# Graph attention on one core: another order for the first batch and another end for the last

## The chip, the core and the metric

The kernel runs on one core of one Trainium2 chip. The metric is device time in microseconds, the median over runs of the same program. Engines are named as in the profile: PE is the matmul engine (TensorE) and PEld its weight loads, DVE is VectorE, ACT is ScalarE, POOL is GpSimd, and SP is the engine that here only issues transfers.

## The reference

There are 16 batches (B) of 1024 rows (N) with 256 features (D), and an adjacency matrix for each batch, 0 or 1 as drawn here and symmetric. Two layers follow each other, each with a residual and a layernorm:

```python
# layer 0, for entries of adj that are 1 (the others give sigmoid(-max) = 0)
e     = leaky_relu(einsum('bid,bjd->bij', x * a0, x), 0.2)
alpha = where(adj == 1, sigmoid(e), 0)
x     = layernorm(x + alpha @ x + bias)
# layer 1
H = x @ W;  s = H @ a[:256];  d = H @ a[256:]
e = where(adj != 0, exp(-leaky_relu(s[:, None] + d[None, :], 0.2)), 0)
x = layernorm(x + elu((e @ H) / rowsum(e)))
```

## The kernel before

The work for one batch is cut into 8 tiles of 128 rows. A batch passes through two slots of the program: in slot b the kernel makes the scores and the layer 0 sum of batch b, and the layer 1 sum of batch b - 1. The order of the instructions is written out by hand (the scheduler is off), so each engine takes its instructions in the order of the Python text, and waits only for data and for buffers.

For layer 0 the score matrix before masking is symmetric, so only its upper part is multiplied. `strip(b, jt)` multiplies the rows of tile jt with all columns from tile jt on (PE, line 208), in chunks of at most 512 columns; ACT applies two tanh to each chunk (lines 216 and 217) and DVE keeps the greater (line 218) in `tb`. `finish(b, jt, c0, c1)` masks the strip with the adjacency (DVE, line 224) and adds 2 on the diagonal block (POOL, line 234), which carries the residual. The lower part comes from the upper one. In batch 0 `mirror(b, jt)` does it by transposes on PE (line 263) that DVE reads from PSUM and masks (line 265); in later batches `dump`, `gather` and `mask` do it by a DVE transpose and two transfers over DRAM. `sum0(b, t)` multiplies the masked scores with x for tile t (line 315), and DVE evicts the sum and takes its statistics (lines 323, 276 and 277). After four tiles `center` makes the reciprocal root of the variance with a power and one Newton step on POOL (lines 283 to 300), and `scale0` normalizes the rows on ACT (line 304).

Layer 1 needs the normalized rows transposed. `save_x1` writes half of them to DRAM, `fetch_x1` reads them back in blocks by eight transfers (line 113), and `turn_x1` finishes the transpose on DVE (line 352). `project` multiplies with W (line 376), extended by two columns that `make_Wx` computes from W and a (lines 165 and 166). `weights(b, m)` makes one row block e of the attention (DVE, line 420), `sum1` multiplies it (PE, line 427), `elu` and `add` make the elu, the residual and the statistics (lines 443 to 456), `scale1` normalizes and `store` writes out.

For batch 0 the transposed x comes from PE: `transpose_x` transposes x (line 189), DVE copies the result (line 191) and ACT multiplies a second copy by a0 (`acol`, line 192). For the other batches `load_blocks` reads x in blocks (eight transfers on SP) and `turn_x` finishes on DVE (line 179) and ACT (line 180). The buffer of batch 1's transposed x is the one that held `a_bc`, which `make_Wx` reads.

PSUM is cut into three pools: `ps_e` (3 buffers, the score chunks), `ps_t` (2 buffers, transposes) and `ps_acc` (3 buffers, sums).

In the first slot of the kernel before, all four transposes of x by halves come first, then strips 0 to 3 with their mirrors 0 to 3, then `make_Wx`, and then the sums, each followed by one of strips 4 to 7. Transfers are issued by SP (x, the blocks, DRAM traffic and stores) and by POOL (the adjacency, which changes type on the way).

At the end of the last batch, tiles 0 to 3 of layer 1 are summed together as the weights become ready, then tiles 4 to 7 one by one. The last three tiles' roots are taken on POOL. Before the last store each engine reads a flag that says whether the data had only zeros and ones in the adjacency (line 659); if so, it jumps over a second, general program (line 1005), and the engines meet at the end (line 1040).

Of the kernel before, what the change touches and what calls it, by code (L numbers as in the profile page):

```python
# [9 lines left out]
F32 = mybir.dt.float32  # L10
# [4 lines left out]
ALU = mybir.AluOpType  # L15
# [3 lines left out]
P = 128  # L19
# [10 lines left out]
def one_kind_pass(  # L30
# [53 lines left out]

    def load_x(b, pieces=1):
        xs[b] = two.tile([P, NT, D], F32, tag="x", name=f"x_{b}")
        rows = x[b].rearrange("(t p) d -> p t d", p=P)
        n = NT // pieces
        for g in range(pieces):
            nc.sync.dma_start(xs[b][:, ts(g, n), :], rows[:, ts(g, n), :])  # L90

# [37 lines left out]


    acol = const.tile([P, ND], F32, tag="acol", name="acol")
    with nc.allow_non_contiguous_dma(reason="a column of 256"):
        nc.sync.dma_start(acol, a0.rearrange("(c p) o -> p (c o)", p=P))
    load_x(0, 2)
    ident = const.tile([P, P], F32, tag="ident", name="ident")
# [3 lines left out]
    minus1 = const.tile([P, 1], F32, tag="minus1", name="minus1")  # L139
    nc.vector.memset(minus1, -1.0)  # L140
    ones = const.tile([P, 1], F32, tag="ones", name="ones")
    nc.vector.memset(ones, 1.0)
# [16 lines left out]

    def make_Wx():  # L160

        for c in range(ND):
            wprod = one.tile([P, 2, D], F32, tag="tmp", name=f"wprod_{c}")
            for s in range(2):
                nc.vector.tensor_tensor(wprod[:, s, :], Wx[:, c, 2:], a_bc[:, ts(s, D)], ALU.mult)
            nc.vector.tensor_reduce(Wx[:, c, 0:2], wprod, AX.X, ALU.add)

# [13 lines left out]

    def transpose_x(b, g, c):
        if g == 0 and c == 0:
            new_xT(b)
            xas[b] = one.tile([P, ND, N], F32, tag="xa", name=f"xa_{b}")
        pool, tag = (ps_t, "t") if g == 0 else (ps_e, "e")
        pt = pool.tile([P, HT, P], F32, tag=tag, name=f"pxT_{b}_{g}_{c}")
        for t in range(HT):
            nc.tensor.transpose(pt[:, t, :], xs[b][:, g * HT + t, ts(c, P)], ident)  # L189
        flat = pt.rearrange("p t q -> p (t q)")  # L190
        nc.vector.tensor_copy(xTs[b][:, c, ts(g, HALF)], flat)
        nc.scalar.mul(xas[b][:, c, ts(g, HALF)], flat, acol[:, c : c + 1])

# [112 lines left out]
    x1s, mv0s, r0s = {}, {}, {}  # L306

    def sum0(b, t):
        if t == 0:
            x1s[b] = two.tile([P, NT, D], F32, tag="x1", name=f"x1_{b}")  # L310
            mv0s[b] = small.tile([P, NT, 2], F32, tag="mv0", name=f"mv0_{b}")
            r0s[b] = []
        acc = ps_acc.tile([P, D], F32, tag="acc", name=f"acc0_{b}_{t}")
        for jt in range(NT):
            nc.tensor.matmul(  # L315
                acc,
                lhsT=als[b][:, jt, ts(t, P)],
                rhs=xs[b][:, jt, :],
                start=(jt == 0),
                stop=(jt == NT - 1),  # L320
            )
        y = x1s[b][:, t, :]
        nc.vector.scalar_tensor_tensor(y, acc, 0.5, bias_bc, ALU.mult, ALU.add)  # L323
        stats(y, mv0s[b][:, t, :], f"0_{b}_{t}")
        if t % HT == HT - 1:
            g = t // HT
            r0s[b] += center(mv0s[b][:, ts(g, HT), :], f"0_{b}_{g}")
# [107 lines left out]
    def elu(b, t, acc):  # L435
# [10 lines left out]
        if (b, t) == (B - 1, NT - 1):  # L446
            nc.vector.tensor_scalar(hs[b, t], acc[:, 0:D], rinv, 0.0, ALU.mult, ALU.max)
        else:
            nc.scalar.activation(hs[b, t], acc[:, 0:D], AF.Relu, scale=rinv)  # L449
        nc.scalar.activation(ys[b][:, t, :], acc[:, 0:D], AF.Exp, scale=rinv)  # L450

    def add(b, t):

        y = ys[b][:, t, :]
        nc.vector.scalar_tensor_tensor(y, y, 1.0, hs[b, t], ALU.min, ALU.add)
        nc.vector.scalar_tensor_tensor(y, y, -1.0, x1s[b][:, t, :], ALU.add, ALU.add)
        stats(y, mv1s[b][:, t, :], f"1_{b}_{t}")
# [3 lines left out]

    def store(b, t0, n):
        rows = out[b].rearrange("(t p) d -> p t d", p=P)
        nc.sync.dma_start(rows[:, ds(t0, n), :], ys[b][:, ds(t0, n), :])

# [4 lines left out]

    for g in range(2):
        for c in range(ND):
            transpose_x(0, g, c)
    strip(0, 0)
    for jt in range(HT):
        if jt < HT - 1:
            strip(0, jt + 1)
        finish(0, jt, 0, HALF)
        mirror(0, jt)
    make_Wx()  # L480
    load_x(1)
    new_xT(1)
    load_blocks(xTs[1], x[1], 0, N)
    for t in range(NT):
        sum0(0, t)
        if t < HT:
            finish(0, t, HALF, N)
            strip(0, t + HT)
        if 1 <= t <= HT:
            finish(0, t + HT - 1)  # L490
            if t < HT:
                mirror(0, t + HT - 1)
        if t in (4, 5):
            scale0(0, 2 * t - 8)
            scale0(0, 2 * t - 7)
        if t == 5:
            save_x1(0, 0)
            fetch_x1(0, 0)
        if t in (5, 6):
            turn_x(1, t - 5)  # L500
        if t < CHECKS:
            check_adj(0, t)

    for b in range(1, B):
# [29 lines left out]
        if not last:  # L534
            load_x(b + 1)
            new_xT(b + 1)
            load_blocks(xTs[b + 1], x[b + 1], 0, N)
# [24 lines left out]
        for t in range(NT):  # L562
# [8 lines left out]
            if last and t == 7:  # L571
                weights(b, 1)
            if t >= 1:
# [24 lines left out]
    last, done = B - 1, B - 2  # L598
    r1s[last] = []
    n_first = 4  # L600
    first = [acc1(last, t, *((ps_e, "e") if t < 3 else (ps_t, "t"))) for t in range(n_first)]
    for m in range(NT):
        if m >= 2:
            weights(last, m)
# [14 lines left out]
    for t in range(NT):  # L619
# [9 lines left out]
        elu(last, t, acc)  # L629
        if 1 <= t < NT - 1:  # L630
            add(last, t - 1)
        if t == 5:
            nc.vector.tensor_copy(flag, total)
        if t == 6:
            add(last, t)
        if t in (4, 6):
            r1s[last] += center(mv1s[last][:, ds(0 if t == 4 else 3, 3), :], f"1_{last}_{t}")
        if t == 6:
            r1s[last] += center(mv1s[last][:, 6:7, :], f"1_{last}_6")
        for q in range(2 * t - 6, 2 * t - 4) if 3 <= t < 7 else []:  # L640
            scale1(done, q)
            if q in (3, 7):
                store(done, q - 3, HT)
        if t == 6:
            for q in range(3):
                scale1(last, q)
            store(last, 0, 3)

    t = NT - 1
    add(last, t)  # L650
    for q in range(3, t):
        scale1(last, q)
        if q == 5:
            store(last, 3, 3)
        elif q == 6:
            store(last, 6, 1)
    mv = mv1s[last][:, t : t + 1, :]
    r = rstd(mv, f"1_{last}_{t}")
    n_bad = nc.values_load(
        flag, min_val=0, max_val=P, skip_runtime_bounds_check_because="a number of partitions"  # L660
    )
    y = ys[last][:, t, :]
    nc.vector.tensor_scalar(y, y, mv[:, 0, 0:1], r, ALU.subtract, ALU.mult)
    store(last, t, 1)
    return n_bad
# [378 lines left out]
```

## Time and profile before

| | us |
|---|---|
| median of 3 runs | 1286.6 |
| lowest and highest of them | 1285.33, 1298.05 |
| the profiled execution, its own time | 1284.06 |
| span of its trace | 1282.3 |
| PE busy | 1258.7 (98%) |
| DVE, ACT, POOL busy | 923.6, 651.9, 294.5 |
| first transpose on PE starts | 5.39 |
| first strip on PE starts | 8.54 |
| first strip of the second slot starts | 56.86 |
| last store is issued | 1273.74 |

The span runs from the first to the last instruction of the program; the profiled execution's own time is 1.8 us longer, for what lies around it. Times in the trace count from the start of the span. A row of the timeline gives the start, the duration, the engine, the line, the operation and its tiles, how many were merged, and in brackets how long the engine had been idle and what ended the wait. A letter q behind an engine's name means its sequencer, which issues transfers and handles waits and jumps.

### The profile page before, as it was taken

To read this page: it belongs to the slowest core of one execution; us is meant where nothing else is said; L and a number is where in the kernel's file an instruction comes from. 1 tells how busy PE (TensorE), PEld (TensorE's weight loads), DVE (VectorE), ACT (ScalarE), POOL (GpSimd) and SP (SyncE) were. 2 spreads that over 40 slices of the span, in tenths; PEclk is the share of its full clock that TensorE was granted. 3 is DMA by queue.
4 is the path that set the end of the run, shared out by engine and by line. 5 is a ranking of instruction groups with operands and counts; after the bars stand their busy time and mean duration, and the time that the engine had idled before them with its cause. 6 is when DMAs were issued, how large, how long until landed. Compare 5 with 4: busy or idle time off the path is not lost.

```text
span 1282.3 us, 17435 instructions
## 1 busy us (share of the span) xinstructions
PE 1258.7 (98%) x5453; PEld 1021.8 (80%) x5453; DVE 923.6 (72%) x1999; ACT 651.9 (51%) x1461; POOL 294.5 (23%) x606
## 2 busy tenths in 40 slices
PE   7999999999999999999999999999999999999995
PEld 5778787887878878788787878878788787887884
DVE  5585877858678686886868768686786868768564
ACT  4544545457354564544545444564545645446424
POOL 2212231212212122221222312222121221212213
PEclk9999999999999999999999999999999999999998
DMA  9388484885948769386694858958487593866201
GB/s 215 69 176 147 88 199 89 178 177 100 200 84 193 147 130 197 75 184 138 140 207 89 194 95 176 179 104 190 90 194 153 123 198 77 190 137 135 81 16 69
DMA packets 604421, 180.25 MB, mean 141 GB/s; under 512 B 481960, under 2 KB 586912, under 8 KB 604320
## 3 DMA queue, kind: packets, MB, share of 16 engines
q1 hardware_dynamic: 583728, 137.56, 49.3%
q0 software_dynamic: 20592, 41.48, 18.3%
q8 instruction: 46, 0.75, 0.2%
q14 instruction: 55, 0.45, 0.1%
HBM read 151.91 MB, written 60.62 MB: 166 GB/s over the span
## 4 chain that ended last, share of the span: by engine, by line
PE 93%; issue 4%; POOL 1%; DVE 0%; DMA 0%; ACT 0%; SPq 0%; POOLq 0%
PE acc L315 34%; PE acc L427 30%; PE pe L208 19%; PE pH L376 8%; POOL r L285 1%; DMA x<-in_x 0%; PE pxT L189 0%; PE pal L263 0%; POOL ve L283 0%; DVE e L420 0%; PE prow L402 0%; POOL mr L300 0%; POOL n L288 0%; POOL n L289 0%; POOL n L290 0%
## 5 line engine op out<-in xcount | busy, mean ns | idle before, releaser
L427 PE MATMUL acc<-H,e 128*128 128x257 f32 x2048 | 448.8, 380 | 0.6 <-DVE e L420 0.6
L315 PE MATMUL acc<-x,al 128*128 128x256 f32 x2048 | 445.5, 379 | 0.0
L427 PEld LDWEIGHTS acc<-H,e 128*128 128x128 f32 x2048 | 387.7, 189 | 58.5 <-DVE e L420 1.3
L315 PEld LDWEIGHTS acc<-x,al 128*128 128x128 f32 x2048 | 387.6, 190 | 52.6 <-issue 0.5
L208 PE MATMUL pe<-xa,xT 128*128 128x384 f32 (+3 forms) x768 | 267.5, 486 | 0.0
L208 PEld LDWEIGHTS pe<-xa,xT 128*128 128x128 f32 x768 | 141.5, 189 | 86.4 <-issue 45.5
L304 ACT ACTIVATE x<-x,mr,r 128x256 f32<-128x256 f32 x128 | 69.2, 592 | 224.5 <-POOL mr L300 224.5
L420 DVE SCALAR_TENSOR_TENSOR e<-p,pq,adj 128x1024 f32<-128x1024 f32 x128 | 159.7, 1270 | 19.3 <-DMA p<-p_row 16.3
L283 POOL TENSOR_SCALAR ve<-mv 128x4 f32<-128x4 f32 (+3 forms) x51 | 17.8, 349 | 677.2 <-DVE mv L277 671.9
L449 ACT ACTIVATE h<-acc,rinv 128x256 f32<-128x256 f32 x127 | 59.7, 470 | 185.7 <-DVE rinv L444 168.1
L216 ACT ACTIVATE tb<-pe 128x512 f32<-128x512 f32 (+1 forms) x192 | 94.3, 491 | 111.5 <-PE pe L208 81.2
L443 DVE TENSOR_SCALAR rinv<-acc 128x1 f32<-128x1 f32 x128 | 20.1, 157 | 160.7 <-PE acc L427 160.7
L121 ACT ACTIVATE junk<-adj,minus 128x2048 bf16<-128x2048 bf16 x64 | 127.4, 1990 | 0.0
L218 DVE TENSOR_TENSOR tb<-tb,low 128x512 f32<-128x512 f32 (+1 forms) x192 | 103.6, 545 | 32.5 <-ACT low L217 32.1
L376 PE MATMUL pH<-Wx,x1T 128*128 128x258 f32 x512 | 126.6, 381 | 0.0
L376 PEld LDWEIGHTS pH<-Wx,x1T 128*128 128x128 f32 x512 | 97.2, 190 | 36.0 <-issue 14.3
L234 POOL TENSOR_TENSOR al<-ident,al 128x128 f32<-128x128 f32 x128 | 68.0, 531 | 225.6 <-DVE al L224 225.3
L224 DVE SCALAR_TENSOR_TENSOR al<-tb,adj 128x512 f32<-128x512 f32 (+7 forms) x132 | 97.5, 738 | 5.0
L323 DVE SCALAR_TENSOR_TENSOR x<-acc,bias_bc 128x256 f32<-128x256 f32 x128 | 53.9, 421 | 57.9 <-PE acc L315 57.8
L217 ACT ACTIVATE low<-pe 128x512 f32<-128x512 f32 (+1 forms) x192 | 93.0, 485 | 0.0
L255 DVE SCALAR_TENSOR_TENSOR al<-al,adj 128x512 f32<-128x512 f32 (+3 forms) x150 | 76.4, 534 | 20.6 <-DMA al<-mir 20.6
L240 DVE STREAM_TRANSPOSE tb<-tb 128x896 f32<-128x896 f32 (+6 forms) x105 | 74.7, 712 | 3.6
(66 smaller groups left out, 904.4 us busy)
## 6 DMA issues: line engine op xcount, KB each, us to landing
adj<-in_adjT POOLq DMA_DIRECT2D x30, 1024.0 KB, 9.5
x_rows<-x SPq DMA_DIRECT2D x31, 512.0 KB, 3.5
x1T<-x_rows SPq DMA_DIRECT2D x248, 64.0 KB, 2.5
x<-in_x SPq DMA_DIRECT2D x15, 1024.0 KB, 5.9
xT<-in_x SPq DMA_DIRECT2D x120, 128.0 KB, 3.4
out<-y SPq DMA_DIRECT2D x30, 512.0 KB, 4.3
p<-p_row POOLq DMA_DIRECT2D x15, 512.0 KB, 4.5
mir<-tb SPq DMA_DIRECT2D x60, 112.0 KB, 2.4
```

Of the source, the lines that this page charges most:

```text
L121: nc.scalar.activation(junk, rows, AF.Square, bias=minus1, scale=2.0, accum_out=chk[:, b * CHECKS + n : b * CHECKS + n + 1],)
L208: nc.tensor.matmul(pe[:, 0:w], lhsT=xTs[b][:, c, ts(jt, P)], rhs=xas[b][:, c, ds(jt * P + o, w)], start=(c == 0), stop=(c == ND - 1),)
L216: nc.scalar.activation(tb[:, ds(o, w)], pe[:, 0:w], AF.Tanh, scale=0.5)
L217: nc.scalar.activation(low[:, 0:w], pe[:, 0:w], AF.Tanh, scale=0.5 * SLOPE)
L218: nc.vector.tensor_tensor(tb[:, ds(o, w)], tb[:, ds(o, w)], low[:, 0:w], ALU.max)
L224: nc.vector.scalar_tensor_tensor(als[b][:, jt, c0:c1], tbs[b, jt][:, c0 - jt * P : c1 - jt * P], 1.0, adjs[b, jt // HT][:, jt % HT, c0:c1] ...
L240: nc.vector.transpose(tb, tb)
L255: nc.vector.scalar_tensor_tensor(v, v, 1.0, rows, ALU.add, ALU.mult)
L315: nc.tensor.matmul(acc, lhsT=als[b][:, jt, ts(t, P)], rhs=xs[b][:, jt, :], start=(jt == 0), stop=(jt == NT - 1),)
L376: nc.tensor.matmul(pt, lhsT=x1Ts[b][:, c, ts(t, P)], rhs=Wx[:, c, :], start=(c == 0), stop=(c == ND - 1),)
L420: nc.vector.scalar_tensor_tensor(es[b][:, m, :], p_bcs[b], pqs[b][:, m, 1:2], adjs[b, m // HT][:, m % HT, :], ALU.mult, ALU.min)
L427: nc.tensor.matmul(acc, lhsT=es[b][:, m, ts(t, P)], rhs=Hs[b][m], start=(m == 0), stop=(m == NT - 1),)
```

## The change

The change has four parts.

1. x of batch 0 is loaded in four quarters instead of two halves. Quarters 0 and 2 are issued by SP and quarters 1 and 3 by ACT, and they come before the load of acol, which was SP's first transfer. `transpose_x` works by quarters, in PSUM buffers of all three pools.
2. The first slot is ordered anew. Strips 0 to 2 and mirrors 0 and 1 come first; from there on each tile's sum is followed by the strip three tiles ahead and the finish and mirror two tiles ahead. `sum0` is divided into `multiply0` (PE) and `end0` (eviction and statistics). `make_Wx` works for one half of W at a time and follows sums 0 and 1, and the block loads of batch 1 come behind it. `turn_x(1, 0)` and `turn_x(1, 1)` come after sums 4 and 5 instead of 5 and 6.
3. In the last batch, weights 1 to 3 are made before the last `add` of batch 14; before it was only weight 1.
4. The end: tiles 3 to 5 are centered one tile earlier, each group behind its own tile. The roots of tiles 6 and 7 are taken together on ACT (`Sqrt`), refined on DVE, and both tiles are scaled on DVE. For tile 7 the residual is added to the first half of elu, so that one addition follows the exponential instead of two. Both tiles go out in one store, which ACT issues.

```diff
-        for g in range(pieces):
-            nc.sync.dma_start(xs[b][:, ts(g, n), :], rows[:, ts(g, n), :])
+        for g, queue in enumerate(queues):
+            queue.dma_start(xs[b][:, ts(g, n), :], rows[:, ts(g, n), :])
...
+    load_x(0, [nc.sync, nc.scalar, nc.sync, nc.scalar])
     acol = const.tile([P, ND], F32, tag="acol", name="acol")
     with nc.allow_non_contiguous_dma(reason="a column of 256"):
         nc.sync.dma_start(acol, a0.rearrange("(c p) o -> p (c o)", p=P))
-    load_x(0, 2)
...
+    def transpose_x(b, g):
+
+        if g == 0:
             new_xT(b)
             xas[b] = one.tile([P, ND, N], F32, tag="xa", name=f"xa_{b}")
+        for c in range(ND):
+            pool, tag = ((ps_t, "t"), (ps_acc, "acc"), (ps_acc if c else ps_e, "acc" if c else "e"), (ps_t, "t"))[g]
+            pt = pool.tile([P, 2, P], F32, tag=tag, name=f"pxT_{b}_{g}_{c}")
+            for t in range(2):
+                nc.tensor.transpose(pt[:, t, :], xs[b][:, 2 * g + t, ts(c, P)], ident)
+            flat = pt.rearrange("p t q -> p (t q)")
+            nc.vector.tensor_copy(xTs[b][:, c, ts(g, 2 * P)], flat)
+            nc.scalar.mul(xas[b][:, c, ts(g, 2 * P)], flat, acol[:, c : c + 1])
...
-    for g in range(2):
-        for c in range(ND):
-            transpose_x(0, g, c)
+    for g in range(NT // 2):
+        transpose_x(0, g)
     strip(0, 0)
-    for jt in range(HT):
-        if jt < HT - 1:
-            strip(0, jt + 1)
+    strip(0, 1)
+    for jt in range(2):
         finish(0, jt, 0, HALF)
         mirror(0, jt)
-    make_Wx()
-    load_x(1)
-    new_xT(1)
-    load_blocks(xTs[1], x[1], 0, N)
+        if jt == 0:
+            strip(0, 2)
+    load_x(1, [nc.sync])
     for t in range(NT):
-        sum0(0, t)
+        multiply0(0, t)
+        if t + 3 < NT:
+            strip(0, t + 3)
+        if t < 2:
+            finish(0, t + 2, 0, HALF)
+        elif t + 2 < NT:
+            finish(0, t + 2)
+        if t + 2 < NT - 1:
+            mirror(0, t + 2)
         if t < HT:
             finish(0, t, HALF, N)
-            strip(0, t + HT)
-        if 1 <= t <= HT:
-            finish(0, t + HT - 1)
-            if t < HT:
-                mirror(0, t + HT - 1)
+        end0(0, t)
+        if t < 2:
+            make_Wx(t)
+        if t == 1:
+            new_xT(1)
+            load_blocks(xTs[1], x[1], 0, N)
+        if 1 <= t <= CHECKS:
+            check_adj(0, t - 1)
         if t in (4, 5):
             scale0(0, 2 * t - 8)
             scale0(0, 2 * t - 7)
+            turn_x(1, t - 4)
         if t == 5:
             save_x1(0, 0)
             fetch_x1(0, 0)
-        if t in (5, 6):
-            turn_x(1, t - 5)
-        if t < CHECKS:
-            check_adj(0, t)
...
             if last and t == 7:
-                weights(b, 1)
+                for m in range(1, 4):
+                    weights(b, m)
...
+    def root(t):
+        nc.scalar.activation(warm, ones, AF.Sqrt)
+        v = mv1s[last][:, t : t + 2, 1]
+        r = const.tile([P, 2], F32, tag="root", name="root")
+        nc.scalar.activation(r, v, AF.Sqrt, bias=eps)
+        nc.vector.reciprocal(r, r)
+        n = const.tile([P, 2], F32, tag="newton", name="newton")
+        nc.vector.scalar_tensor_tensor(n, v, EPS, r, ALU.add, ALU.mult)
+        nc.vector.scalar_tensor_tensor(n, n, -0.5, r, ALU.mult, ALU.mult)
+        nc.vector.scalar_tensor_tensor(r, n, 1.5, r, ALU.add, ALU.mult)
+        return r
...
-        if t in (4, 6):
-            r1s[last] += center(mv1s[last][:, ds(0 if t == 4 else 3, 3), :], f"1_{last}_{t}")
-        if t == 6:
-            r1s[last] += center(mv1s[last][:, 6:7, :], f"1_{last}_6")
+        if t in (4, 5):
+            r1s[last] += center(mv1s[last][:, ds(3 * t - 12, 3), :], f"1_{last}_{t}")
...
+    add(last, NT - 1)
+    r = root(6)
     n_bad = nc.values_load(
         flag, min_val=0, max_val=P, skip_runtime_bounds_check_because="a number of partitions"
     )
-    y = ys[last][:, t, :]
-    nc.vector.tensor_scalar(y, y, mv[:, 0, 0:1], r, ALU.subtract, ALU.mult)
-    store(last, t, 1)
+    for q in (6, 7):
+        y = ys[last][:, q, :]
+        nc.vector.tensor_scalar(
+            y, y, mv1s[last][:, q, 0:1], r[:, q - 6 : q - 5], ALU.subtract, ALU.mult
+        )
+    store(last, 6, 2, nc.scalar)
```

## The prediction

> **What bounds the kernel now.** I read the busy table first, then the chain, then busy time by stage, then the timeline of the two ends that the change touches.
>
> ```profile
> PE 1258.7 (98%) x5453; PEld 1021.8 (80%) x5453; DVE 923.6 (72%) x1999; ACT 651.9 (51%) x1461; POOL 294.5 (23%) x606
> ...
> PE 93%; issue 4%; POOL 1%; DVE 0%; DMA 0%; ACT 0%; SPq 0%; POOLq 0%
> ```
>
> The stage table gives for each stretch its length, the busy time of PE, PEld, DVE, ACT and POOL, the granted clock, the DMA share and GB/s:
>
> ```profile
> 8.54:56.86 48.32, 46.73 (x206) 35.78 (x205) 29.91 (x68) 23.99 (x41) 6.70 (x16) 1.00 0.79 155
> ...
> 63.30:1241.80 1178.50, 1177.52 (x5105) 958.67 (x5103) 865.21 (x1856) 607.72 (x1381) 264.82 (x530) 1.00 0.70 143
> ...
> 1266.70:1282.30 15.60, 0.00 (x1) 0.00 (x0) 2.68 (x8) 2.97 (x6) 5.00 (x20) 0.64 0.30 102
> ```
>
> PE is idle for only 1282.3 - 1258.7 = 23.6 us. The stage table says where: almost nothing in the 1178 us in the middle, 15.6 us after the last matmul, the rest in the first slot. The change touches only the ends, so all it can win lies there, and a gain of 1% (12.9 us, about what a measurement of this kernel can tell from no change) would need over half of all PE idle time back. Now the places, from the timeline:
>
> ```profile
> 0.73 0.44 SPq L133 DMA_DIRECT2D acol<-in_a  x1
> ...
> 5.39 3.32 PE L189 MATMUL pxT<-ident,x 128*128 128x128 f32 x16 [5.39 <-DMA x<-in_x]
> ...
> 8.54 6.61 PE L208 MATMUL pe<-xa,xT 128*128 128x512 f32 x16
> ...
> 23.61 0.63 PE L263 MATMUL pal<-ident,tb 128*128 128x128 f32 x4 [1.59 <-DVE al L265]
> ...
> 59.89 1.25 DVE L352 STREAM_TRANSPOSE x1T<-x1T 128x1024 f32<-128x1024 f32 x1 [1.73 <-DMA x1T<-x_rows]
> ...
> 63.30 1.03 PE L376 MATMUL pH<-Wx,x1T 128*128 128x258 f32 x4
> ...
> 1241.80 17.63 PE L427 MATMUL acc<-H,e 128*128 128x257 f32 x80 [0.64 <-DVE e L420]
> ```
>
> The reader should see four waits: for the first x (5.39), for DVE to free a mirror's PSUM (1.59), for a weight row e (0.64), and one that costs PE nothing: DVE waits for x1T, but its transpose ends at 61.14, 2.16 us before PE needs it for pH at 63.30.
>
> ```profile
> 0.72 1.28 ACT L145 ACT_TABLE_LOAD   x1 [0.72 <-PEq L1032]
> ...
> 1267.71 0.47 ACT L450 ACTIVATE y<-acc,rinv 128x256 f32<-128x256 f32 x1 [0.69 <-DVE h L447]
> ...
> 1271.30 0.22 POOL L283 TENSOR_SCALAR ve<-mv 128x1 f32<-128x1 f32 x1
> ...
> 1273.30 0.41 DVE L663 TENSOR_SCALAR y<-y,mv,r 128x256 f32<-128x256 f32 x1 [3.52 <-POOL r L291]
> ```
>
> And of SP's own waits in the last 13 us (total, times, longest):
>
> ```profile
> SPq L1040 <- DMA adj<-in_adjT: 3.1, 1, 3.1
> ```
>
> Behind the last matmul (E = 1266.70) the chain runs over POOL: the statistics are ready at 1269.78, POOL starts the root only at 1271.30 because tile 6's stands before it, DVE scales at 1273.30, SP stores at 1273.74 (E+7.04).
>
> **Start, before the first strip.** acol's issue leaves the head of SP's queue: x is issued 0.49 us earlier (1.22 to 0.73), and in quarters. x's first half landed at 5.25, the second at 6.72, after streaming at 380 to 390 GB/s from 3.6 to 6.0 us, so a second queue saves issue slots and no streaming; the last quarter should land at 6.72 - 0.49 = 6.2, the first near 4.5. PE starts near 4.6 instead of 5.39. But acol now stands behind two quarters on SP's ring, and every xa multiply needs it. It lands between 6.2 (with the last quarter) and 7.8 (bias, behind x, landed 1.54 us after it); I take 6.7, nearer the former, as it moves 1 KB. Four multiplies must follow before the first strip: 3 spacings of 0.37 and 0.47 (rows L449 to L450, L386), so the strip starts at 8.3 to 8.4 instead of 8.54: **+0.2**, ends -0.9 (acol at 7.8) and +0.8 (acol early; strip 3.15 after PE's start, as before). The smaller copies are covered by that wait; ACT's two issues (0.5 each) delay only the table load, ready by 3.
>
> Here a rule speaks against it. The transposes started 0.213 us apart until 8.19 and 0.11 after, though the profile's granted clock says 1.00 throughout: PE ran at half rate for its first 2.8 us. By that row it is at full rate by 8.3. The Trainium skill (TensorE: Matmul & The Clock Gate, Part 1) wants about 3.4 us of sustained activity; PE now pauses for acol, so by the rule the strips could run at half rate to about 11 us, costing (11 - 8.3)/2 = 1.4. I take the row and keep the 1.4 for the range.
>
> **First slot.** Times from the first strip's start S. Up to the second mirror the order is the old one, so its durations hold: mirror 1 ends on DVE at S+12.9, PE is free at S+10.45. Before, PE then ran strip 3 and waited 1.59 us for a mirror's PSUM. Now sum 0 (3.46 us) and strips alternate, and that wait goes. What is late next: sum 4 needs finish(3) of the upper half, which DVE does only behind strip 6. From strip 6's end: 0.2 to ACT, max at +0.94, finish(5), mirror 5, then finish(3) ends at +2.74 (rows 39.57 to 40.78, then 0.66). PE arrives there at +1.52 (pal_5 0.22, three of eight sum steps 1.3): a **new wait of 1.3 us**. PE's work is 46.15 (strips 9 x 1.72, mirrors 28 x 0.108, sums 27.64), so slot 1 starts at S+47.46, before at S+48.32: 0.86 gained.
>
> It is not kept. make_Wx, needed to free the buffer for the next slot's xT, moves between sums; it ends at S+28.0 (before S+19.3), and SP's eight block loads start there. First half landed 9.5 us after its start: S+37.5. DVE reaches turn_x(0) at S+39.8, so it isn't blocked, but the row scaling of tiles 2 and 3 now stands behind its xa multiply on ACT: turn ends 41.05, multiply 42.25, scaling 43.3, save_x1 at S+43.35 (before S+40.97). Save to landing 2.93, eight fetches 7.3, DVE transpose 1.25, as in the trace: x1T ready at S+55.0. PE wants pH at 47.46 + 6.44 = S+53.9. So pH starts at S+55.05, before S+54.76: **-0.3**, and the whole head is level (-0.1). Slot 1's DVE then lags PE more, but it had 2.1 us idle between 60 and 80; strips wait on ACT's two low buffers, which by the same durations stay a tile ahead.
>
> **Last weights.** Steps 1 to 3 are now made before add(6). e2 is ready at 1240.3 instead of 1241.74; PE wants it at 1240.98. The gap of 1240.77 to 1241.80 shrinks by 0.82 and a ragged 0.1 behind it; in return add(6) runs later, e6 still ends at 1247.97 and PE now meets it at 1247.90, a wait of 0.13. **+0.75** (0.5 to 0.9).
>
> **End.** From E: rinv and reciprocal to 0.40, h to 0.92 (0.48), the new add of x1 (0.42) to 1.38 beside ACT's exp, which as before starts behind h: 1.02 to 1.49. One add instead of two: 1.95; statistics 2.63. ACT: table load 1.49 to 2.78 (1.28), warm, root 3.05. DVE: reciprocal and three small steps at 0.2 each: 3.87; its flag load (0.54, now on the path; before it lay beside POOL's root) 4.25; two scalings of 0.41 overlapping: 5.1. ACT stores at E+5.15: 1.9 earlier. Queued before exp on ACT: three scalings of tiles 3 to 5, free about E+1.0, just in time.
>
> The rule against it: the Trainium skill (ScalarE: Activation LUTs, What ACT_TABLE_LOAD costs) puts a switch at 1283 ns plus a drain of about 1380 ns. The trace has one load, 1.28, with the next activation 0.01 behind it, but at the start with nothing to drain. By the row the store goes at E+5.15, by the rule at E+6.5. I take the row: the program has no drain there.
>
> What ends the kernel is behind the store. POOL took the skip of the other pass at 1273.65, and its own chain (resumed at 1276.32, gap to 1278.65, a semaphore step, a drain to 1281.43) ran 8.6 us to the end; SP, done with the store's landing (1275.98) at 1276.37, waited 3.1 us for it. With no root left on POOL its skip comes at about E-0.1, its chain is over at E+7.7. Then the store's landing decides: two tiles are 256 KB, between 128 KB (2.25) and 384 KB (3.4): 2.6, so E+7.75. SP's steps after it take 1.2 as seen (0.38 + 0.81), or 3.4 if it pauses after landing as POOL did at 1276.43; no row tells, I take 2.3. Last barrier 0.8: E+10.9, against 15.58: **+4.7** (3.3 by the drain rule; 3.6 to 5.8 by SP's pause).
>
> **Sum.** -0.1 + 0.75 + 4.7 = 5.3 us. Span 1282.3 to 1277.0, that execution's time 1284.06 to 1278.8. The median 1286.6 stands 2.5 above that execution; I move it by the same 5.3: **1281.3**, likeliest case's own range 1278.5 to 1283.5.
>
> **Rivals.**
> - The end is a fixed tail behind the last store: only 1.9 comes back there, total 2.5, 1284.1. For it: store and POOL's skip lay 0.1 apart, so the trace cannot separate them. Against: SP waited 3.1 us for POOL, not for the store.
> - The head pays too: acol early (S 0.8 earlier) and x1T not last (0.86 kept), total 5.4 + 1.7 = 7.1, 1279.5. For: x1T is late by 1.1 us only, on durations added over 40 us. Against: every link of it has a row.
> - Slower: turn_x(0) blocks DVE. One mechanism: the block loads land late, DVE waits with finish(7), evictions and statistics behind it, and x1T moves with it. It costs one for one once they land over 2.3 us late, and outweighs the gain from 7.6 late; 10 late gives 1289.0. Against: fewer transfers run beside them than before (adj had landed by 34.3).
>
> **How the numbers follow.** Forecast 0.55, fixed tail 0.16, head pays 0.24, slower 0.05. 1277.5 to 1285.0 takes in the first three with drain and half-rate costs and about 1 us between runs. Over 1% faster has no case (0.03 for what I missed); over 1% slower needs the third at its worst: 0.03; within 1%: 0.94.
>
> **What would show it.** The first strip near 8.3, waiting for acol; a PE gap of 1.3 us inside sum 4; DVE waiting for x1T and pH near 63.4; no gap at the third weight; a second table load of 1.28 and the store near E+5.2; the end near E+10.9. A first strip before 7.9 or pH before 62 makes the head wrong; an end over 13 us behind E, the tail.

## The result, and the profile after

The changed kernel takes **1277.61 us** (median of 11 runs, 1276.72 to 1283.05), the kernel before 1285.74 beside it (11 runs). The medians differ by 8.1 us (0.63%). The ratio of the comparison, which is that of the means, is 0.992 with a 95% interval of 0.9892 to 0.9948; it lies further from 1 than the ratio of the medians (0.9937) because four runs of the kernel before took 1290 to 1298 us. Run again later, the changed kernel took 1277.93 beside 1285.35 (ratio 0.9941, 0.9919 to 0.9963). The forecast was 1281.3, 5.3 us faster: the direction was right and the gain too small. The result lies below the range of the likeliest case (1278.5 to 1283.5) and at the fast edge of the whole range (1277.5 to 1285.0).

The profiled execution took 1277.0 us with a span of 1275.0; before it was 1284.06 and 1282.3. The two spans divide at two events that the change doesn't move past one another, the start of pH (layer 1's first multiplication) and the end of the last matmul:

| stretch, us | before | after | gain | forecast |
|---|---|---|---|---|
| program start to pH | 63.30 | 62.62 | 0.68 | -0.1 |
| pH to the end of the last matmul | 1203.40 | 1202.71 | 0.69 | 0.75 |
| the last matmul to the end | 15.57 | 9.66 | 5.91 | 4.7 |

From the page of the changed kernel, busy times and the chain that ended last:

```profile
PE 1259.0 (99%) x5453; PEld 1024.4 (80%) x5453; DVE 925.1 (73%) x2011; ACT 651.6 (51%) x1467; POOL 291.1 (23%) x592
...
PE 98%; DVE 0%; ACT 0%; DMA 0%; issue 0%; DVEq 0%; ACTq 0%
```

PE is as busy as before (1258.7). The 4% of "issue" and POOL's 1% are gone from the chain: what was won is idle time of PE. The stage table, with columns as for the kernel before:

```profile
8.21:56.18 47.97, 46.73 (x205) 36.06 (x205) 29.77 (x70) 24.18 (x43) 6.38 (x16) 1.00 0.81 152
62.62:1241.80 1179.18, 1178.83 (x5111) 962.24 (x5110) 867.07 (x1857) 605.91 (x1380) 265.55 (x530) 1.00 0.75 143
1265.33:1275.00 9.67, 0.00 (x0) 0.00 (x0) 3.65 (x13) 3.15 (x7) 0.00 (x0) 0.65 0.36 124
```

The first slot is 0.35 shorter (48.32 before), the middle has 0.35 of PE idle instead of 0.98, and POOL does nothing in the last stretch, where it worked 5.0 us before. The timeline of the start:

```profile
0.72 1.02 ACTq L90 DMA_DIRECT2D x<-in_x  x2
...
1.72 0.46 SPq L134 DMA_DIRECT2D acol<-in_a  x1
...
4.77 3.65 PE L192 MATMUL pxT<-ident,x 128*128 128x128 f32 x16 [4.77 <-DMA x<-in_x]
...
6.75 3.02 ACT L195 ACTIVATE xa<-pxT,acol 128x256 f32<-128x256 f32 x8 [3.47 <-DVE xT L194]
...
8.21 1.72 PE L211 MATMUL pe<-xa,xT 128*128 128x512 f32 x3
```

PE starts 0.62 earlier and runs without a gap into the first strip. The timeline of the first slot's second half:

```profile
43.00 2.43 PE L324 MATMUL acc<-x,al 128*128 128x256 f32 x10 [1.24 <-DVE al L227]
...
51.66 0.39 SPq L352 DMA_DIRECT2D x_rows<-x  x1
54.64 4.38 SPq L113 DMA_DIRECT2D x1T<-x_rows  x8
56.18 6.61 PE L211 MATMUL pe<-xa,xT 128*128 128x512 f32 x16
61.00 1.25 DVE L363 STREAM_TRANSPOSE x1T<-x1T 128x1024 f32<-128x1024 f32 x1 [3.51 <-DMA x1T<-x_rows]
...
62.62 0.60 PE L387 MATMUL pH<-Wx,x1T 128*128 128x258 f32 x2
```

The wait of 1.59 at a mirror is gone and a wait of 1.24 inside sum 4 has come. DVE ends x1T's transpose at 62.25, and PE reaches pH at 62.62 with no gap: 6.44 us behind slot 1's start, exactly as before (63.30 - 56.86). The weights and the end:

```profile
1237.77 12.46 PE L438 MATMUL acc<-H,e 128*128 128x257 f32 x55
...
1265.36 0.16 DVE L454 TENSOR_SCALAR rinv<-acc 128x1 f32<-128x1 f32 x1 [0.57 <-PE acc L438]
...
1266.33 0.47 ACT L464 ACTIVATE y<-acc,rinv 128x256 f32<-128x256 f32 x1
1266.82 1.28 ACT L626 ACT_TABLE_LOAD   x1
...
1268.23 0.28 ACT L629 ACTIVATE root<-mv,eps 128x2 f32<-128x2 f32 x1
...
1269.78 0.74 DVE L696 TENSOR_SCALAR y<-y,mv,root 128x256 f32<-128x256 f32 x2 [0.48 <-DVE root L635]
1270.55 0.40 ACTq L479 DMA_DIRECT2D out<-y  x1
```

The first line is one unbroken row of matmuls where the kernel before waited 0.64 us (1241.15 to 1241.80) for weight row e. From the root on, every step is there that the forecast named. SP's waits in the last 10 us (total, times, longest):

```profile
SPq L1040 <- SPq L1040: 5.5, 3, 3.2
...
SPq L1075 <- PEq L1075: 0.7, 2, 0.5
```

SP now waits for the landing of the store (3.14 us, to 1273.02) and no more for POOL; the row of 3.1 us that stood there before is gone. By the sequencers' own records, SP's steps behind the landing end at 1274.18, ScalarE has got over its jump at 1274.03, and POOL was done at 1271.39.

### The profile page after: what moved, and what is told of

The parts are those of the page before. It is cut to its first block, busy times and chain, and to the rows that moved or that the text cites. A ratio compares the mean times of both kernels' runs of the same rounds, so it can differ in the third digit from the quotient of the medians.

```text
span 1275.0 us, 17435 instructions
## 1 busy us (share of the span) xinstructions
PE 1259.0 (99%) x5453; PEld 1024.4 (80%) x5453; DVE 925.1 (73%) x2011; ACT 651.6 (51%) x1467; POOL 291.1 (23%) x592
## 4 chain that ended last, share of the span: by engine, by line
PE 98%; DVE 0%; ACT 0%; DMA 0%; issue 0%; DVEq 0%; ACTq 0%
PE acc L438 35%; PE acc L324 35%; PE pe L211 19%; PE pH L387 9%; DMA x<-in_x 0%; PE pxT L192 0%; PE pal L266 0%; PE prow L413 0%; ACT y L307 0%; PE pp L406 0%; ACT L626 0%; DVE al L227 0%; PE px1T L370 0%; ACT y L464 0%; DVE y L696 0%
## 5 line engine op out<-in xcount | busy, mean ns | idle before, releaser
L286 POOL TENSOR_SCALAR ve<-mv 128x4 f32<-128x4 f32 (+2 forms) x49 | 16.8, 343 | 663.6 <-DVE mv L280 659.5
L334 DVE SCALAR_TENSOR_TENSOR x<-acc,bias_bc 128x256 f32<-128x256 f32 x128 | 53.9, 421 | 44.3 <-PE acc L324 44.0
L464 ACT ACTIVATE y<-acc,rinv 128x256 f32<-128x256 f32 x128 | 59.8, 467 | 42.4 <-DMA out<-y 42.4
```

## Experiments

Each run is compared with the kernel before on its own chip. Differences of less than about 2 us are read from the traces at the three stretches of the table above, since the medians carry a disturbance of some microseconds that the sixth group explains. Each such reading is one trace. The end repeats well: it is 9.62 to 9.79 us long in the eight traces that have the changed kernel's end as it stands, and 15.57, 16.05 and 16.20 in the three that have the old one. The stretch to pH repeats less well, for the reason in the fifth group.

### 1. Parts alone

`end_only` is the kernel before with part 4, `head_only` the kernel before with parts 1 and 2.

> The kernel before with part 4 (the new end) alone. Theory A (the parts add up): the last matmul still ends near 1266.7, the program ends 9.7 us behind it instead of 15.6, so the gain is 5.9 us. Theory B (the tail is fixed behind the last store): only the store's advance of 1.9 us comes back.

> The kernel before with parts 1 and 2 alone (start and first slot); weights and end stay. Theory A (read from the trace after): PE starts pH near 62.6 instead of 63.3, the gap of 0.8 at the third weight stays, the end stays 15.6 behind the last matmul: gain 0.7 us. Theory B (the forecast, x1T late): pH near 63.4, gain 0 or a loss of 0.1.

`end_only`: the last matmul ends at 1268.43 and the program at 1278.22, **9.79** behind it; the lowest of 20 runs is 1278.58, against 1284.48 for the kernel before. The tail's gain is the end's alone, 5.8 us, and theory B (1.9) is out. Its median is only 1282.8, with runs up to 1292: see group 6. The head in this run was slower (pH at 64.89) though only one small memset was added to it: see group 5.

`head_only`: pH at 62.93 (0.37 earlier than before, 1.24 us of new wait included), a median 1.2 us below. Theory A's sign holds, its size only about half. A PE gap of 2.6 us at 821 us, again of group 6's kind, spoils its span, and its end, the old one, took 16.20. Both kernels keep the gap at the third weight (0.64 and 0.65), so the 0.69 of the middle stretch is part 3's. Parts 1 and 2 were not run apart from each other, nor part 3 alone.

### 2. What ended the kernel before: POOL made late again, and SP given the store back

```diff
 r = root(6)
+held = const.tile([P, 2], F32, tag="held", name="held")
+nc.gpsimd.tensor_scalar(held, r, 1.0, None, ALU.mult)        # pool_late
...
-store(last, 6, 2, nc.scalar)
+store(last, 6, 2)                                            # sp_store
```

> The changed kernel with one small operation on POOL that reads the refined root, so that POOL reads its flag and jumps only about 4.5 us behind the last matmul instead of 0.8 ahead of it; the store is not touched. Theory A (POOL's own chain of 8.6 us from jump to end was what ended the kernel before): the end moves from 9.7 to about 13.3 behind the last matmul, 3.5 us slower than the changed kernel. Theory B (the end hangs on the store alone): no change, below 0.3.

> The changed kernel with its last store issued by SP instead of ACT; POOL stays early. In the trace before, SP stood still from 1276.37 to 1279.49, behind the store's landing. Theory A (as the forecast said, SP waited there for POOL): with POOL early SP goes on at once, no change, below 0.3 us. Theory B (that pause is SP's own and follows its jump: 5.3 us from the jump to the next step, as ACT and DVE stand still for about 3 us behind theirs): SP jumps near 5.7 us behind the last matmul, resumes near 11.0, and the end comes near 12.2 behind it, 2 to 2.5 us slower than the changed kernel.

The last stretch of `pool_late`, and then of `sp_store`:

```profile
1265.24:1276.42 11.18, 0.00 (x0) 0.00 (x0) 3.65 (x13) 3.15 (x7) 0.22 (x1) 0.62 0.33 108
```

```profile
1275.73:1285.68 9.95, 0.00 (x1) 0.00 (x0) 3.65 (x13) 3.16 (x7) 0.00 (x0) 0.68 0.36 121
```

With its 0.22 us operation POOL jumps at 1269.86 and ends the kernel: 1.5 us later, though the store goes out at the same time (1270.45, 5.2 behind the last matmul). So POOL's chain can end the kernel, and does so without touching the store; but it took 6.6 us from jump to end, not 8.6, and the expected 3.5 us were too many. `sp_store` loses 0.3 us: the store goes out 5.22 behind the last matmul as in the changed kernel, but in this trace it landed 2.75 us later and not 2.45. SP jumps only at 1281.42, waits for the landing, and goes on at once. SP has no pause of its own behind the landing, so the 3.1 us of the kernel before were a wait for POOL, as the forecast said. (Behind its jump SP did stand still for 2.4 us in `end_only`, off the path, and for 0.4 in every other trace.)

Most of part 4's gain comes from taking POOL out of the end. An estimate from these traces: in the kernel before the last store landed at E+9.28; with the 1.16 us of SP's steps and the 0.81 of the last barrier that the changed kernel shows, it would have ended at about E+11.3 without POOL. That is 4.3 of the 5.9 us; the earlier store brings the rest.

### 3. The two microseconds that POOL's chain was shorter

```diff
 nc.gpsimd.memset(power, -0.5)
+pad = const.tile([P, NT], F32, tag="pad", name="pad")
+for _ in range(8):
+    nc.gpsimd.memset(pad, 0.0)
```

> The kernel before with eight tiny memsets more on POOL at its start, off the path; they only shift POOL's later instructions by eight places. Before, POOL paused twice behind its jump: 2.67 us, and 2.22 us more after two instructions, though the semaphores it then tested belong to loads long done. Theory A (the second pause is a second load of instructions that depends on where the code lies): the second pause goes, the end comes 13.4 us behind the last matmul instead of 15.6, 2.2 us faster than before. Theory B (the pause waits for something in the program): 15.6 stays.

The last stretch of `before_pad`, and under it SP's wait there for what it had waited 3.1 us before:

```profile
1272.63:1286.19 13.56, 0.01 (x1) 0.00 (x0) 2.68 (x8) 2.98 (x6) 5.01 (x20) 0.70 0.34 117
```

```profile
SPq L1043 <- DMA adj<-in_adjT: 0.9, 1, 0.9
```

Eight memsets at the start of the program take **2.0 us** off its end. POOL's second pause behind the jump (1276.43 to 1278.65 before) is gone, and SP's wait, which the profile puts down to an old load of adj, shrinks with it. It really is for POOL: in the kernel before, in `before_pad` and in `pool_late` SP goes on 0.57 to 0.58 us after the start of the same step of POOL's, which the records call INC_SWDGE_SEM. The lowest run is 1282.61 against 1284.60. The traces `head_only` and `before_store_early`, which have the old end too, do have the second pause (2.29 and 2.33). The memsets touch nothing that the end uses; what they move is the place of POOL's later instructions, so that pause most likely depends on where the code lies. That it is a second load of instructions fits this but is not shown: two transfers of the trace's instruction queue start inside the pause (1276.83 and 1276.95), but two start at the like place in `before_pad` (1282.74 and 1283.06), where there is no pause, and the trace does not say for which engine they are. In the median (1285.38 against 1285.93) group 6's disturbance hides most of it.

### 4. The end: one step off its path

The flag is read by all engines ahead of tile 7's `elu`, where DVE waits for PE anyway:

```diff
+if t == NT - 1:
+    n_bad = nc.values_load(flag, ...)
 elu(last, t, acc)
...
 r = root(6)
-n_bad = nc.values_load(flag, ...)
```

> The changed kernel with the flag read by every engine ahead of tile 7's elu instead of between the root and the two scalings. In the trace after, DVE's flag read took 0.54 us (1269.14 to 1269.68) between the last Newton step (1269.29) and the first scaling (1269.78). Theory A (the chain root, scalings, store, landing sets the end): store near E+4.75 instead of E+5.22, end near E+9.2 instead of E+9.66, 0.45 us faster. Theory B (the jumps of POOL or DVE and their steps set it): no change.

```profile
1272.20:1281.37 9.17, 0.00 (x0) 0.00 (x0) 3.65 (x13) 3.15 (x7) 0.00 (x0) 0.62 0.39 131
```

This last stretch of `flag_early` is 0.49 us shorter, the store 4.76 behind the last matmul instead of 5.22. So what sets the end of the changed kernel lies behind the two scalings. Two chains start there: the store, its landing and SP's steps, and ScalarE's own jump behind the store. They end within 0.1 us of each other in the changed kernel, and this run moves both. In `sp_store` ScalarE jumps 2.4 us earlier and the end does not come earlier, so the store's chain is enough to set it.

### 5. The head: which wait is late next

`no_wait4` finishes strip 3's upper half ahead of strip 5; `no_wait4_save` also puts `turn_x` behind `save_x1`.

```diff
+        if t == 3:
+            finish(0, t, HALF, N)
...
-        if t < HT:
+        if t < 3:
             finish(0, t, HALF, N)
...
         if t in (4, 5):
             scale0(0, 2 * t - 8)
             scale0(0, 2 * t - 7)
-            turn_x(1, t - 4)
         if t == 5:
             save_x1(0, 0)
             fetch_x1(0, 0)
+        if t in (5, 6):
+            turn_x(1, t - 5)                     # no_wait4_save only
```

> The changed kernel with the finish of strip 3's upper half put ahead of strip 5's finish, so that sum 4 needn't wait for it. Theory A (x1T is ready just ahead of pH and binds next): the 1.24 us gap in sum 4 goes, slot 1 starts near 55.0, but x1T's transpose still ends near 62, so pH comes near 62.0: gain 0.3 to 0.8 us of the 1.24. Theory B (x1T follows and nothing binds): the whole 1.2 us.

> The kernel no_wait4, and turn_x of batch 1 put behind save_x1 again, so that its xa multiplies don't stand ahead of the row scalings on ScalarE. Theory A (those two multiplies hold x1T back): save_x1 is issued 1.2 us earlier, near 50.4, x1T is ready near 61.0, pH starts near 61.4, 1.2 us earlier than in the changed kernel. Theory B (the fetches set x1T, by what else is under way on the queues): x1T stays near 62.

The timeline of `no_wait4`:

```profile
42.32 2.42 PE L324 MATMUL acc<-x,al 128*128 128x256 f32 x10 [0.29 <-DVE al L227]
...
60.07 1.25 DVE L363 STREAM_TRANSPOSE x1T<-x1T 128x1024 f32<-128x1024 f32 x1 [3.26 <-DMA x1T<-x_rows]
...
61.94 1.03 PE L387 MATMUL pH<-Wx,x1T 128*128 128x258 f32 x4
```

The wait shrinks from 1.24 to 0.29, and all of that 0.95 arrives at pH: pH is 0.68 earlier in a run whose second strip matmul started 0.27 later. x1T is ready at 61.31, 0.63 ahead of pH: freeing DVE moves it along, so theory B holds and x1T does not bind. `no_wait4_save` confirms it from the other side: x1T's margin grows to 1.09 and pH gains nothing. (It comes at 62.48, 0.54 later than in `no_wait4`, and by 0.54 later the fourth strip matmul starts: PE's start, below, was slower in that trace.) In all seventeen traces pH starts 6.44 us behind slot 1 (to 0.01), and x1T is ready by then.

Next, PE's own start. `warm_pe` gives PE work before x has landed; `warm_acol` adds acol between SP's two quarters of x.

```diff
+heat = ps_acc.tile([P, 2, P], F32, tag="acc", name="heat")
+for _ in range(14):
+    nc.tensor.transpose(heat[:, 0, :], ident, ident)
 for g in range(NT // 2):
     transpose_x(0, g)
```

> The changed kernel with 14 transposes of the identity on PE (into a PSUM tile that nobody reads) ahead of the first x. In the traces so far PE ran at half rate for 2.9 to 5.4 us after its first matmul, in whichever instruction that fell. Theory A (the half rate counts from PE's first activity): the dummies take the slow time, the x transposes go at 0.11 us, the first strip starts near 7.3 (then acol, landed at 6.7, and two xa multiplies decide) and runs at 0.43 a matmul from its start: slot 1 and pH 1.0 to 1.4 us earlier than in the changed kernel, and so the end. Theory B (the half rate ends at a fixed time of the program, or only real data ends it): strip near 8.2, no gain. x1T must then be ready by 61.4, which it follows if it hangs on the strip's start and not on the loads.

> The kernel warm_pe with acol issued between SP's two quarters of x instead of behind them. In warm_pe the x transposes ran at full rate, but ScalarE's first xa multiply waited for acol until 6.6 us, the last quarter's transposes waited for the PSUM that it frees until 7.14, and slot 1 started no earlier. Theory A (acol is what binds behind the half rate): xa starts near 5.3, the first strip near 7.1 instead of 7.9, slot 1 and pH 0.7 us earlier than in warm_pe. Theory B (ScalarE's and VectorE's chain over the strips sets slot 1, whatever the start): strip earlier, pH within 0.2 of 62.55.

The timeline of `warm_pe`, then that of `warm_acol`:

```profile
4.49 2.13 PE L192 MATMUL pxT<-ident,x 128*128 128x128 f32 x12
6.61 3.03 ACT L195 ACTIVATE xa<-pxT,acol 128x256 f32<-128x256 f32 x8 [3.34 <-DMA acol<-in_a]
7.14 0.80 PE L192 MATMUL pxT<-ident,x 128*128 128x128 f32 x4 [0.52 <-ACT xa L195]
7.87 2.41 PE L211 MATMUL pe<-xa,xT 128*128 128x512 f32 x5
```

```profile
1.22 0.46 SPq L137 DMA_DIRECT2D acol<-in_a  x1
...
4.39 3.22 PE L197 MATMUL pxT<-ident,x 128*128 128x128 f32 x16
5.58 3.45 ACT L200 ACTIVATE xa<-pxT,acol 128x256 f32<-128x256 f32 x8 [2.30 <-DVE xT L199]
7.45 2.74 PE L216 MATMUL pe<-xa,xT 128*128 128x512 f32 x6
```

Warm alone wins nothing at pH (62.55): ScalarE waits for acol until 6.6 and PE for ScalarE. With acol early as well, pH comes at **61.59**, 1.03 us earlier than in the changed kernel. Two things stand side by side at the start: the half rate at which PE does its first matmuls, and acol; taking away one shows the other. acol early without the warm-up was not run.

How long the half rate lasts differs from execution to execution. The tile view gives the durations of single strip matmuls (count: min/median/max in ns, then first and last start), first in the kernel before, then in `no_wait4_save`, in nearly the same stretch; the granted clock reads 1.00 in both:

```profile
L208 PE MATMUL pe<-xa,xT x6: 592/592/595, 8.5 to 10.7; 128*128 128x512 f32 x6
```

```profile
L211 PE MATMUL pe<-xa,xT x4: 593/1011/1062, 8.1 to 10.6; 128*128 128x512 f32 x4
```

Before, every strip matmul was at full rate, 0.43 us apart; here three of four were at half. By the spacing of matmuls the half rate lasted 2.9 us from PE's first transpose in the kernel before, 4.0 in the changed kernel, 4.9 in `sp_store`, 5.8 in `end_only` and 6.0 in `before_pad`; in `after_again`, the same kernel as the changed one, at most 2.8. That is why the unchanged head of `end_only` and `before_pad` reaches pH only at 64.89 and 65.10.

### 6. Gaps in the middle, and the medians

In seven of the first fourteen traces PE stands still for 1.1 to 5.1 us once or twice in the middle, on either kernel. The timeline of `sp_store` at one of them:

```profile
667.51 0.47 ACT L464 ACTIVATE y<-acc,rinv 128x256 f32<-128x256 f32 x1 [7.74 <-DMA out<-y]
...
668.02 0.43 DVE L469 SCALAR_TENSOR_TENSOR y<-y,h 128x256 f32<-128x256 f32 x1 [6.18 <-ACT y L464]
...
668.04 1.02 PE L438 MATMUL acc<-H,e 128*128 128x257 f32 x2 [3.12 <-ACT y L464]
```

`y` has one buffer. A slot's first exponential writes into it and must wait until the store of the batch before has landed, which SP issued (657.45) only some 2 us before the exponential could have started. PE has three accumulators and feels the wait late: in the nine gaps seen, the gap is 4.5 to 5.5 us shorter than ScalarE's wait. To test this, the rows of batch b - 2 are scaled in pairs ahead of sums 2 to 5 (counted from 0), so that the store goes out two sums earlier:

```diff
-            if done >= 0:
-                scale1(done, t)
-                if t in (3, 7):
-                    store(done, t - 3, HT)
+            for q in (2 * t - 4, 2 * t - 3) if done >= 0 and 2 <= t < 6 else []:
+                scale1(done, q)
+                if q in (3, 7):
+                    store(done, q - 3, HT)
```

> The changed kernel with batch b - 2's rows scaled two tiles at a time behind sums 2 to 5 (before: one tile behind each of the sums 0 to 7), so that its second store is issued two sums, some 7 us, earlier. Theory A (the first exponential of a slot waits for that store to land, since y has one buffer): ScalarE's pause there, 1.7 to 4.2 us in the trace after and up to 10.6 in others, shrinks below 1 us, no PE gap of over 1 us is left in the middle, and runs far above the lowest become rare: median within 0.5 us of the lowest, 0.5 to 1 us below the changed kernel's; the lowest stays within 0.5. Theory B (loading of instructions, or the DMA traffic itself): pauses and spread stay.

> The kernel before with the same earlier store. Theory A (the store's landing): its median comes down by 0.5 to 1 us to about 1284.7, near its lowest, and then the two medians differ by about as much as the traces (7.3). Theory B: 1285.4 to 1285.9 as in the comparisons so far.

ScalarE's waits (total, times, longest) in the changed kernel, in `sp_store` and in `store_early`:

```profile
ACT y L464 <- DMA out<-y: 42.4, 14, 4.2
```

```profile
ACT y L464 <- DMA out<-y: 49.5, 14, 8.1
```

```profile
ACT y L464 <- DMA out<-y: 19.5, 10, 3.1
```

The waits don't fall below 1 us, which I had expected, but they fall below what PE can take up: no gap of over 1 us in the middle is left in either kernel with the early store, and the spread is gone: 1277.16 to 1277.90 in 6 runs, 1284.83 to 1286.39 in 14. The longest of these waits is 2.8 to 3.2 us in the three traces with the early store and 4.2 to 10.6 in the other fourteen. The edit moves the scalings along with the store, and does not part the two; but it leaves ScalarE's instructions at the same number (1467), and the waits that shrank are those for the store. The medians I had expected to fall don't: 1277.47 (against 1277.61 and 1277.93) and **1285.44** for the kernel before. That answers where the 8.1 came from. Free of gaps, the two kernels differ by 8.0 us in the median and by 7.9 in the spans (1283.1 and 1275.2: 0.80 to pH, 0.71 in the middle, 6.42 at the end). The profile before was simply a quick execution, 1.4 below this median: one of the shortest half rates seen, and an end 0.5 us shorter than in `before_store_early` (15.57 against 16.05).

> The changed kernel once more, beside the others on the same chip. Theory A (its 7.3 us are pH 0.7, weights 0.7, end 5.9): the same readings within 0.3 us, except for the half rate of PE at the start, which lasts 3 to 5 us from run to run. Where a run is 3 us or more above the lowest, a gap in the middle should show, as in the traces that had one.

It gave pH at 62.49 and an end 9.62 behind the last matmul, within 0.15 of the first trace, and a gap of 1.72 at 977 us, behind the same exponential.

### 7. A faster version

`all_three` joins `warm_acol`, `no_wait4` and `flag_early`; `all_four` adds the early store.

> The changed kernel with PE warmed up, acol between the quarters, strip 3's upper half finished ahead of strip 5, and the flag read early. If the terms add: pH near 61 (0.95 from the wait in sum 4, 0.3 to 0.7 from the start), end 9.2 us behind the last matmul: 1.7 to 2.1 us faster than the changed kernel, where no stall in the middle hides it. If x1T binds behind them: pH no earlier than 61.7, gain 1.2 to 1.4.

> The kernel all_three with the same earlier store. Theory A: lowest near 1274.5 as in all_three, median within 0.5 of it. Theory B: median near 1275.2 with runs up to 1280, as in all_three.

```profile
60.93:1263.62 1202.69, 1202.34 (x5218) 979.81 (x5216) 885.67 (x1914) 619.85 (x1407) 279.15 (x554) 1.00 0.73 141
1263.62:1272.82 9.20, 0.00 (x0) 0.00 (x0) 3.66 (x13) 3.15 (x7) 0.00 (x0) 0.61 0.39 129
```

`all_three` takes 1275.18 us (pH at 60.84), `all_four`, whose last two stretches are shown, **1274.80** (1274.68 to 1275.04), 2.7 below `store_early` on the same chip; against the kernel before the ratio is 0.9912 (0.9898 to 0.9927). The terms nearly add: 0.95 and 1.03 at pH alone, 1.78 together in `all_three`, and 0.48 at the end.

## Why the prediction was right or wrong

**What failed, in sum.** The forecast's gain of 5.3 us is 2.8 short. The end gained 1.2 more than forecast (SP's steps after the landing), the head 0.8 more (above all because x1T was ready earlier), and the step from one trace to the median missed another 0.7. The rest, 0.1, is within the medians' scatter.

**Start: right sum, wrong reason.** The strip started at 8.21, forecast 8.3 to 8.4, and acol landed at 6.66, forecast 6.7. But the strip did not wait for acol: 16 transposes at 0.213 from 4.77 end there by themselves. In `warm_pe`, where the rate rose earlier, and in `flag_early`, where acol landed only at 7.42, acol did bind (the first xa multiply waited for it until 6.6 and 7.5).

**The half rate: a row of one execution taken for a constant.** By the row of before PE was to be at full rate by 8.3; the changed kernel's half rate reached 0.5 us into the first strip and cost 0.27, and in other runs up to 1.3. The Trainium skill (TensorE: Matmul & The Clock Gate, Part 1), with about 3.4 us of sustained activity, lies inside the 2.8 to 6.0 measured, and the 1.4 us estimated from it was the better bound. The reason given for the 1.4, a pause of PE for acol, did not come about in that trace. No run shows what sets the length.

**First slot: two right steps, one wrong.** The old wait went, and the new one was 1.24 (forecast 1.3; its two times, +2.74 and +1.52, give 1.22). The failing step is "x1T ready at S+55.0": counted from the strip's start at 8.21 it was ready at S+54.0, because the eight fetches, from the first issue to the last landing, took 6.3 us and not the 7.3 of the trace before, where they started here:

```profile
52.50 5.41 SPq L113 DMA_DIRECT2D x1T<-x_rows  x8
```

The save was where the forecast put it (S+43.45 against S+43.35). PE arrived later than forecast too (S+54.4 against S+53.9: the slot's PE work is 46.73, not the sum of 46.15, and the stage table of the kernel before had 46.73 too), so x1T cost nothing, and -0.1 became +0.68. What shortened the fetches is not settled. SP issued them in 4.0 to 4.9 us in the kernels with the new order and in 4.3 to 5.4 with the old one; to x1T's transpose it was 5.8 to 7.0 and 6.2 to 7.4. The 7.4 of the trace before is the longest of all seventeen: it was a draw too, and with it x1T would have been ready only at 63.3, as forecast.

**Last weights: right**, 0.69 for 0.75; both waits were seen (the old gap is gone, and at 1247 two matmuls start 0.1 late each, for the forecast 0.13).

**End: mechanism right, one term mis-sized.** Store at 5.22 (forecast 5.15), landing 2.45 (2.6), last barrier 0.81 (0.8). The table switch cost 1.28 and the next activation came 0.01 later, so the row was right against the Trainium skill's drain of about 1380 ns (ScalarE: Activation LUTs, What ACT_TABLE_LOAD costs). The term that failed is SP's steps after the landing: I took 2.3, between 1.2 and 3.4; they took **1.16**. The 3.4 would have needed a pause of SP's own behind the landing, and `sp_store` shows that there is none; the 1.2 that the trace before showed was right, and it should not have been averaged with the 3.4. That is 1.1 of the 1.2 us.

**From trace to median: a step that failed.** "I move it by the same" took the profile before as a typical execution. Between the two traces the gain is 7.3; between kernels free of gaps it is 8.0, because the profile before was quick at its start and at its end.

**The rivals.** The fixed tail is refuted by `end_only` and `pool_late`. "The head pays too" came nearest in its number (7.1), by luck: the head paid 0.68 and not 1.6, and the rest came from the end. Of its two reasons x1T not being last was the right one. DVE was never blocked by `turn_x(0)` (48.22, on data landed before).

## What to carry to other kernels

Ask of each engine when it is finally free, not only of the one that stores: the end of a program waits for the last of them, and work moved off the slow one can be worth more than a faster store. A duration that comes once in a trace (the half rate at the start, a pause behind a jump, a round of transfers) is one draw; before a sum of tenths rests on it, look for a second occurrence or carry its range. And where runs of one kernel differ by several microseconds, look at waits on a single-buffered tile, whose length is set by a transfer's landing.

## What I had not expected of the hardware

- Behind their jumps POOL, ScalarE and VectorE took 2.4 to 3.4 us to their next step, in all seventeen traces; SP took 0.4, and 2.4 once. In the kernel before POOL had a second pause of 2.2 us after two instructions more, which eight extra instructions elsewhere removed, with 2.0 us of the program's time.
- PE's half rate at a cold start lasted from under 3 to 6.0 us in identical or nearly identical code, at a granted clock of 1.00 in the profile. Identity transposes from 1.35 us on used up 3.0 to 3.1 us of it before PE got x; in these runs it lasted 3.7 to 5.1.
- One 512 KB store under heavy traffic landed about 10 us after its issue in the stalled slot of `sp_store`, which a single buffer turned into 3.1 us of idle PE.
